# Moving convolution pieces, splitting v's operand and shifting the taps' network in a fused Swin block and dynamic convolution

## The chip, the cores and the metric

The kernel runs on one core of one Trainium2 chip. The metric is the device time of one execution in microseconds (us). The kernel before takes 3256.59 us, the median of three runs (3252.11 to 3258.15). The profiled execution has a span of 3259.7 us. All data are float32.

The engines are named as in the profile: PE is TensorE (PEld is its weight load, which overlaps the matmuls), DVE is VectorE, ACT is ScalarE, POOL is GpSimd and SP is SyncE, which here only issues transfers.

## What is computed

Sixteen images of 192 channels and 56x56 points go through two layers. Layer 0 is a shifted-window transformer block. Layer 1 is a depthwise 3x3 convolution whose weights depend on the image's mean.

```python
# layer 0, per image (windows of 7x7, shift 3, 6 heads of 32)
h   = window(roll(layernorm(x), -3))
qkv = h @ qkv_w + qkv_b
p   = softmax(q k^T * scale + rel_bias + mask)
x1  = x + roll(unwindow((p v) @ proj_w + proj_b), 3)
x2  = x1 + gelu(layernorm(x1) @ fc1_w + fc1_b) @ fc2_w + fc2_b
# layer 1, per image
t   = relu(gamma * (mean_hw(x2) @ w1.T - running_mean) * rsqrt(running_var + eps) + beta)
wt  = (t @ w2.T + b2) * causal_mask          # 4 of the 9 taps of each channel are left
out = depthwise_conv3x3(x2, wt) + bias
```

## The kernel before

An image is cut into four steps. A step is two bands of seven rows, one from each half of the image, so a tile `[128, 2, 392]` holds 128 channels of both halves, and a tile `[128, 392]` holds the last 64 channels with the half in the partition. There are 64 steps. The main loop's round `i` does three things at once: the MLP of step `i-2`, the attention of step `i`, and the projections q, k and v of step `i+1`. A round's matmuls come in this order: MLP layer one (`ph`), statistics (`st`), scores (`sc`), q/k (`pq`, `pe`, `pk`), MLP layer two, wide part (`pf`) with the transposes of the probabilities (`pt`) between its slices, values (`po`), MLP layer two, narrow part (`pf1`), projection (`pp`) mixed with v (`pv`).

PSUM is used as four pairs of banks, A, B, C and D, handed from tile to tile. At the end of a round the pairs are renamed, `pairs = [C, B_, D, A]`. A tile's next user waits until the last reader of the tile before has finished. The program is written in order, and each engine runs its own instructions in the order written.

After the fourth step of an image (its last MLP round) the taps `wt` of the image are computed. In the three rounds that follow, its convolution is done in six pieces, two a round. A piece is one ACT instruction (`conv_begin`) and three DVE instructions (`conv_rest`).

```python
def attention_v_out(pvs):                         # v leaves PSUM, block-diagonal
    for blk, pv in enumerate(pvs):
        ...
        for s in range(2):
            for j in range(2):
                for h in range(2):
                    dst = vbd[j * 64 : j * 64 + N, h].rearrange(...)[:, blk, :, s, :, j, :]
                    f = src[s * 64 : s * 64 + N, h, :, :, j, :]
                    if j == 0:
                        nc.vector.tensor_copy(dst, f)     # L450
                    else:
                        nc.scalar.copy(dst, f)            # L452

def residual(i, pp, pp1):
    ...
    for lo, hi, to in rolls:                      # 2 instructions, L578
        nc.vector.scalar_tensor_tensor(xs, q1[:, :, lo:hi], pb[1], xs, ALU.add, ALU.add)
    for a in range(2):                            # 4 instructions, L582
        for lo, hi, to in rolls:
            nc.vector.scalar_tensor_tensor(xs, q0[:, a, :, lo:hi], pb[0], xs, ALU.add, ALU.add)

def mlp_first(i, yn, hid, ks, between):           # ks = (A, B, C, D, A, B)
    def gelu(f):
        nc.scalar.activation(hid[:, f], phs[f][:, :, :T], AF.Gelu, bias=f1b[:, f : f + 1])  # L596
    for f in range(3):
        take(f); long(dsts[f], wf1, cols(f), y0, True)
    for f in range(3):
        short(dsts[f], wf1, cols(f), y1, False); gelu(f)
    for f in range(3, NFC):
        take(f); short(dsts[f], wf1, cols(f), y1, True)
    between()
    for f in range(3, NFC):
        long(dsts[f], wf1, cols(f), y0, False); gelu(f)

def norm_squares(key, i, side, engine):           # with engine = ACT at a round's end
    nc.scalar.activation(s0, v0, AF.Square)       # L243
    nc.scalar.activation(s1, v1, AF.Square)       # L244
    for h in range(2):
        nc.gpsimd.tensor_tensor(s0[p, h], s0[p, h], s1[p], ALU.add)   # L250

def taps_pool(b):
    nc.vector.tensor_reduce(pooled, sums.pop(b), AX.X, ALU.add)
    x0, x1 = images[b]                            # the rows above the halves
    nc.gpsimd.tensor_copy(x0[:, 0, :], x0[:, IMG, :])                 # L650
    nc.vector.tensor_copy(x1[0:64, 0, :], x1[64:128, HALF, :])
    nc.vector.tensor_copy(x1[64:128, 0, :], x1[0:64, HALF, :])
    return pooled

def taps(b, pooled, k):
    pt = banks(f"t_{b}", k)[:, 0]
    for kc in range(2):
        mm(pt[:, 0:RED], pooled[:, kc].broadcast_to([128, 128]), w1t[:, kc], kc == 0, kc == 1)
    nc.vector.tensor_tensor(tt[:, 0], pt[:, 0:RED], bn[:, 0], ALU.mult)   # L661
    nc.vector.tensor_tensor(tt[:, 0], tt[:, 0], bn[:, 1], ALU.add)
    nc.vector.scalar_tensor_tensor(tw, tt..., 0.0, w2n..., ALU.max, ALU.mult)
    nc.vector.tensor_reduce(wt..., tw, AX.X, ALU.add)
    nc.vector.tensor_tensor(wt, wt, b2t, ALU.add)

def conv_begin(b, wt, n):
    nc.scalar.activation(y, images[b][kc][:, lo : lo + PR], AF.Identity,
                         bias=cb[kc], scale=wt[:, kc, 1:2])               # L683

def conv_rest(b, wt, n, y):
    tap(0, ...); tap(2, ...)                      # L698, DVE
    if n in (3, 5):
        nc.vector.tensor_copy(y[p, LAST - 3 * PR, :], ...)                # L707
    tap(3, ...)                                   # L698
    ... nc.sync.dma_start(out[...], y[...])

for i in range(2, NS + 2):                        # a round
    norm1_scale(i + 1, dvs.pop(0), nc.vector)     # 12 DVE instructions
    ...
    def between():
        for b, wt, n in conv_ready(1):            # first piece of the round
            conv_rest(b, wt, n, conv_begin(b, wt, n))
        singles[0] = banks(f"st_{i}", C)
        keys.update(stats_of(i))
        var.append(norm_vars(keys))               # ACT L280, DVE L282 read st
    mlp_first(i - 2, yns.pop(i - 2), hid, (A, B_, C, D, A, B_), between)
    ...                                           # scores, q/k, MLP layer two
    ys = [(*c, conv_begin(*c)) for c in conv_ready(1)]   # second piece of the round
    ...
    pf1 = mlp_narrow(i - 2, hid, A)
    for c in ys:
        conv_rest(*c)
    mlp_out(i - 2, 1, pf1[:, :T])                 # L641
    pp, pp1, p_narrow, p_rest, p_whole = project(i, o, B_, C)
    p_narrow(); p_rest()
    pvs, v_rest, v_whole = attention_v(i + 1, (D, A)); v_rest()
    p_whole(); residual(i, pp, pp1); v_whole()
    if (i - 2) % STEPS == STEPS - 1:              # the image's last MLP round
        convs.append({"b": b, "n": 0, "wt": taps(b, taps_pool(b), C)})
    attention_v_out(pvs)
    norm_squares(f"2_{i}", i, 1, nc.scalar)
    pairs = [C, B_, D, A]
```

Of the kernel before, what the change touches and what calls it, by code (L numbers as in the profile page):

```python
# [8 lines left out]
F32 = mybir.dt.float32  # L9
AF = mybir.ActivationFunctionType  # L10
ALU = mybir.AluOpType
AX = mybir.AxisListType

DIM, HEADS, HD = 192, 6, 32
C0, C1 = 128, 64
IMG = 56
NTOK = IMG * IMG
WS, SHIFT = 7, 3
NWIN = IMG // WS
N = WS * WS  # L20
T = WS * IMG
PW = 64 + N
HALF = IMG // 2
STEPS = NWIN // 2
HID = 4 * DIM
NFC = HID // 128
RED = DIM // 4
# [9 lines left out]
def tile_swin_then_dynamic_conv(  # L37
# [31 lines left out]
    nc = tc.nc  # L69
# [13 lines left out]
    def banks(name, k):  # L83
        return psum.tile([128, 2, 512], F32, tag=f"pair{k}", name=name)
# [6 lines left out]
    def mm(dst, lhs, rhs, start, stop):  # L91
        nc.tensor.matmul(dst, lhs, rhs, start=start, stop=stop, skip_group_check=True)  # L92
# [108 lines left out]


    kbd = one.tile([128, 3, NWIN, 2, N], F32, tag="kbd", name="kbd")
    vbd = const.tile([128, 2, NWIN, HEADS // 2, 64], F32, tag="vbd", name="vbd")
    prob = [
        const.tile([128, 2 * HEADS, 64], F32, tag=f"prob{i}", name=f"prob{i}") for i in range(4)
    ]
# [229 lines left out]
    def attention_v_out(pvs):  # L437

        for blk, pv in enumerate(pvs):
            src = pv.rearrange("p h (w n) -> p h w n", w=2)[:, :, :, 0:DIM]  # L440
            src = src.rearrange("p h w (g j d) -> p h w g j d", j=2, d=HD)
            for s in range(2):
                for j in range(2):
                    for h in range(2):
                        dst = vbd[j * 64 : j * 64 + N, h].rearrange(
                            "p (b w s) g (j d) -> p b w s g j d", b=2, s=2, j=2
                        )[:, blk, :, s, :, j, :]
                        f = src[s * 64 : s * 64 + N, h, :, :, j, :]
                        if j == 0:
                            nc.vector.tensor_copy(dst, f)  # L450
                        else:
                            nc.scalar.copy(dst, f)  # L452

    def attention_scores(i, q4, q2, ks):

# [62 lines left out]
    def attention_weigh(po, po1, wp, prt):  # L518
        for s in range(2):
            w = wp * 2 + s  # L520
            for a, g in ((0, 0), (0, 1), (1, 0), (1, 1), (0, 2), (1, 2)):

                r, k = (g, a) if g < 2 else (a, 2)
                o = po[:, a] if g < 2 else po1
                at = (g if g < 2 else a) * 64
                mm(
                    o[at : at + 64, w * N : (w + 1) * N],
                    vbd[:, a, w, g, :],
                    prt[:, r, k * PW + s * 64 : k * PW + s * 64 + N],
                    True,  # L530
                    True,
                )
# [17 lines left out]

    def project(i, o, k, k1):

        pp, pp1 = banks(f"pp_{i}", k), banks(f"pp1_{i}", k1)[:, 0]

        def narrow():
            for a in range(2):
                mm(pp1[a * 64 : a * 64 + 64, :T], wp0[:, C0:DIM], o[:, a], True, False)

        def rest():
            for a in range(2):  # L560
                p = slice(a * 64, a * 64 + 64)
                mm(pp[:, a, :T], wp1[p], o[p, 2], True, False)

        def whole():
            mm(pp1[:, :T], wp2, o[:, 2], False, True)
            for a in range(2):
                mm(pp[:, a, :T], wp0[:, 0:C0], o[:, a], False, True)

        return pp, pp1, narrow, rest, whole

    def residual(i, pp, pp1):
        v0, v1 = rows_of(i)
        q1 = pp1[:, :T].rearrange("p (r c) -> p r c", c=IMG)
        q0 = pp[:, :, :T].rearrange("p h (r c) -> p h r c", c=IMG)
        rolls = ((0, IMG - SHIFT, SHIFT), (IMG - SHIFT, IMG, 0))
        for lo, hi, to in rolls:
            xs = v1[:, :, to : to + hi - lo]
            nc.vector.scalar_tensor_tensor(xs, q1[:, :, lo:hi], pb[1], xs, ALU.add, ALU.add)  # L578
        for a in range(2):
            for lo, hi, to in rolls:  # L580
                xs = v0[:, a, :, to : to + hi - lo]
                nc.vector.scalar_tensor_tensor(xs, q0[:, a, :, lo:hi], pb[0], xs, ALU.add, ALU.add)  # L582
# [63 lines left out]
    def taps_pool(b):  # L646
        pooled = small.tile([128, 2, 1], F32, tag="pooled", name=f"pooled_{b}")
        nc.vector.tensor_reduce(pooled, sums.pop(b), AX.X, ALU.add)
        x0, x1 = images[b]
        nc.gpsimd.tensor_copy(x0[:, 0, :], x0[:, IMG, :])  # L650
        nc.vector.tensor_copy(x1[0:64, 0, :], x1[64:128, HALF, :])
        nc.vector.tensor_copy(x1[64:128, 0, :], x1[0:64, HALF, :])
        return pooled

    def taps(b, pooled, k):

        pt = banks(f"t_{b}", k)[:, 0]
        for kc in range(2):
            mm(pt[:, 0:RED], pooled[:, kc].broadcast_to([128, 128]), w1t[:, kc], kc == 0, kc == 1)
        tt = small.tile([128, 1, RED], F32, tag="tt", name=f"tt_{b}", bufs=1)  # L660
        nc.vector.tensor_tensor(tt[:, 0], pt[:, 0:RED], bn[:, 0], ALU.mult)  # L661
        nc.vector.tensor_tensor(tt[:, 0], tt[:, 0], bn[:, 1], ALU.add)
        tw = small.tile([128, 2 * NTAP, RED], F32, tag="tw", name=f"tw_{b}", bufs=1)
        nc.vector.scalar_tensor_tensor(
            tw,
            tt.broadcast_to([128, 2 * NTAP, RED]),
            0.0,
            w2n.rearrange("p k t r -> p (k t) r"),
            ALU.max,
            ALU.mult,  # L670
        )
        wt = small.tile([128, 2, NTAP], F32, tag="wt", name=f"wt_{b}")
        nc.vector.tensor_reduce(
            wt.rearrange("p k (t o) -> p (k t) o", o=1), tw, AX.X, ALU.add
        )
        nc.vector.tensor_tensor(wt, wt, b2t, ALU.add)
        return wt
# [51 lines left out]
    def has(i):  # L729
        return 0 <= i < NS  # L730

    def conv_ready(k):

        ready = []
        while k and convs and "wt" in convs[0]:
            c = convs[0]
            ready.append((c["b"], c["wt"], c["n"]))
            c["n"] += 1
            k -= 1
            if c["n"] == 6:  # L740
                convs.pop(0)
        return ready
# [7 lines left out]
    def tail_of(i, o, kp, kv):  # L750

        pvs, v_rest, v_whole = attention_v(i + 1, kv) if has(i + 1) else (None, None, None)
        if o is not None:
            pp, pp1, narrow, rest, whole = project(i, o, kp, 3)
            narrow()
            rest()
        if pvs:
            v_rest()
        if o is not None:
            whole()  # L760
            residual(i, pp, pp1)
        if pvs:
            v_whole()
            attention_v_out(pvs)
        if o is not None:
            norm_squares(f"2_{i}", i, 1, nc.scalar)
# [59 lines left out]
    for c, at, lo, n, be, bias in (  # L826
# [5 lines left out]
        p = slice(at, at + n)  # L832
# [2 lines left out]
    nc.vector.tensor_scalar(qkb[:, 0:1], qkb[:, 0:1], SCALE, None, ALU.mult)  # L835
    nc.vector.tensor_scalar(qkb[0:64, 2:3], qkb[0:64, 2:3], SCALE, None, ALU.mult)
    nc.vector.tensor_scalar(kb, pick, qkb[:, 1:2], None, ALU.mult)
    for t in [kbd, vbd] + prob:
        nc.gpsimd.memset(t, 0.0)
    keys = stats_of(-1)  # L840
    dev = norm_devs(keys)
# [66 lines left out]
    def taps_weights():  # L908
# [30 lines left out]
        nc.vector.tensor_tensor(m, m, s, ALU.mult)  # L939
        nc.vector.tensor_tensor(m, b, m, ALU.subtract)  # L940
        nc.vector.tensor_scalar(s, s, 1.0 / NTOK, None, ALU.mult)

# [30 lines left out]
    for i in range(2, NS + 2):  # L975
        A, B_, C, D = pairs
        keys = {}


        if has(i + 1):  # L980
            norm1_scale(i + 1, dvs.pop(0), nc.vector)
        if (i + 3) % STEPS == 0 and (i + 3) // STEPS < B:
            b = (i + 3) // STEPS
            images[b] = load_x(b, nc.sync)

        def between():
            for b, wt, n in conv_ready(1):
                conv_rest(b, wt, n, conv_begin(b, wt, n))
            singles[0] = banks(f"st_{i}", C)
            keys.update(stats_of(i))  # L990
            if keys:
                var.append(norm_vars(keys))
# [45 lines left out]
        pf = mlp_wide(i - 2, hid, B_, turn)  # L1038
        mlp_out(i - 2, 0, pf[:, :, :T])
        table(AF.Gelu)  # L1040
        ys = [(*c, conv_begin(*c)) for c in conv_ready(1)]
        if 1 in keys:
            yns[i - 1] = norm2_scale(i - 1, dvs.pop(1))
        if has(i + 3):
# [1 line left out]
        if has(i):  # L1046
            o = attention_rows(i, attention_values(i, prts, D, C))
        pf1 = mlp_narrow(i - 2, hid, A)
        for c in ys:
            conv_rest(*c)  # L1050
        mlp_out(i - 2, 1, pf1[:, :T])
        if has(i):
            pp, pp1, p_narrow, p_rest, p_whole = project(i, o, B_, C)
            p_narrow()
            p_rest()
        if has(i + 1):
# [1 line left out]
            v_rest()  # L1058
        if has(i):
            p_whole()  # L1060
            residual(i, pp, pp1)
        if has(i + 1):
            v_whole()
        if (i - 2) % STEPS == STEPS - 1:
            b = (i - 2) // STEPS
            convs.append({"b": b, "n": 0, "wt": taps(b, taps_pool(b), C)})
        if has(i + 1):
            attention_v_out(pvs)
        if has(i):
            norm_squares(f"2_{i}", i, 1, nc.scalar)  # L1070
        pairs = [C, B_, D, A]
    c = convs.pop()
    for n in range(6):
# [75 lines left out]
```

## Time and profile before

| engine | busy us | share of the span |
|---|---|---|
| PE | 3128.8 | 96% |
| DVE | 2155.5 | 66% |
| ACT | 1855.1 | 57% |
| POOL | 1020.4 | 31% |

Round lengths, measured in the timeline from a round's first `ph` matmul to the next round's, repeat with a period of four:

| round | what it holds besides attention and MLP | length, us |
|---|---|---|
| image's last MLP round | the taps' network, no convolution | 48.61 |
| first after it | pieces 0 and 1 | 49.21 |
| second | pieces 2 and 3 | 47.67, in some images 48.28 to 48.41 |
| third | pieces 4 and 5 | 47.67, in some images 48.28 to 48.45 |

In the profile's lists, "idle before" is time in which an engine stood still just before an instruction, and the name after the arrow is what ended that idle time. In the timeline, each row is a run of alike instructions with its start, its duration, the engine, the source line and the tiles as out<-in. In the sums over stretches of time, PEclk is the share of full clock that TensorE was granted.

### The profile page before, as it was taken

Reading aid. Unit: us, or ns where it says so; the run is one execution under the profiler, and the core shown is the slowest. Engines: PE = TensorE matmul, PEld = TensorE weight load, DVE = VectorE, ACT = ScalarE, POOL = GpSimd, SP = SyncE. Lnnn points to the kernel's source line nnn. Section 1 sums busy time; section 2 is a strip of 40 time slices with the busy share of each in tenths; the row PEclk is TensorE's granted clock in tenths of the full one; section 3 lists DMA queues with packets and bytes.
Section 4 is the critical chain, followed back from the end, with each engine's and each line's share of the span. In section 5 each row is a group of like instructions: output and inputs, shape, how many; then the busy total and the mean of one; then the engine's idle time right before and its main releaser. Section 6 shows DMA issues by size and latency. Waiting matters only on the chain.

```text
span 3259.7 us, 64143 instructions
## 1 busy us (share of the span) xinstructions
PE 3128.8 (96%) x26130; PEld 1938.8 (59%) x26130; DVE 2155.5 (66%) x3893; ACT 1855.1 (57%) x2988; POOL 1020.4 (31%) x912
## 2 busy tenths in 40 slices
PE   5699999999999999999999999999999999999996
PEld 3456566666666656666666656666665666666653
DVE  4345666766767676676776766676676767667664
ACT  2445655655655665565665565565565565566552
POOL 4333233233233223333323323323323323323220
PEclk7699999999999999999999999999999999999998
DMA  3001012121111202102111111202111120201101
GB/s 99 12 19 48 20 40 56 31 60 31 33 53 36 61 26 65 31 26 60 37 51 36 54 29 39 55 30 62 31 32 55 36 59 28 65 25 31 26 31 45
DMA packets 79123, 135.35 MB, mean 42 GB/s; under 512 B 21766, under 2 KB 61692, under 8 KB 76908
## 3 DMA queue, kind: packets, MB, share of 16 engines
q1 hardware_dynamic: 77266, 128.54, 14.0%
q8 instruction: 206, 3.38, 0.4%
q0 software_dynamic: 1056, 1.92, 0.3%
q10 hardware_dynamic: 506, 0.79, 0.1%
q14 instruction: 89, 0.73, 0.1%
HBM read 41.25 MB, written 38.54 MB: 24 GB/s over the span
## 4 chain that ended last, share of the span: by engine, by line
PE 89%; DVE 4%; ACT 2%; issue 1%; POOL 0%; DMA 0%; ACTq 0%; DVEq 0%; POOLq 0%
PE ph L92 23%; PE pf L92 22%; PE pv L92 7%; PE pp L92 7%; PE po L92 5%; PE pq L92 4%; PE pt L509 4%; PE sc L92 4%; PE st L92 4%; PE pe L92 4%; PE pk L92 4%; DVE y L698 1%; DVE vbd L450 1%; DVE y L707 1%; ACT vbd L452 1%
## 5 line engine op out<-in xcount | busy, mean ns | idle before, releaser
L92 PE MATMUL ph<-yn,wf 128*128 128x392 f32 (+1 forms) x3072 | 811.4, 501 | 27.3 <-ACT vbd L452 18.8
L92 PE MATMUL pf<-hid,wf 128*128 128x392 f32 (+1 forms) x3072 | 802.8, 494 | 3.5 <-ACT hid L596 2.0
L496 POOL TENSOR_TENSOR prob<-e,tot 113x588 f32<-113x588 f32 x256 | 298.1, 1176 | 1165.8 <-DVE tot L495 1151.3
L92 PEld LDWEIGHTS ph<-yn,wf 128*128 128x128 f32 (+1 forms) x3072 | 425.4, 189 | 384.4 <-issue 91.6
L452 ACT COPY vbd<-pv 49x192 f32<-49x192 f32 x512 | 135.4, 312 | 768.1 <-DVE vbd L450 767.8
L92 PEld LDWEIGHTS pf<-hid,wf 128*128 128x128 f32 (+1 forms) x3072 | 386.4, 164 | 303.6 <-issue 119.9
L698 DVE SCALAR_TENSOR_TENSOR y<-x,wt,y 128x770 f32<-128x770 f32 x288 | 321.0, 1116 | 214.8 <-ACT y L683 208.1
L596 ACT ACTIVATE hid<-ph,f1b 128x784 f32<-128x784 f32 x384 | 336.8, 912 | 127.7 <-PE ph L92 127.3
L250 POOL TENSOR_TENSOR sq<-sq,sq 64x392 f32<-64x392 f32 x256 | 262.9, 1027 | 383.1 <-ACT sq L244 368.6
L347 POOL TENSOR_TENSOR yn<-x,dv 128x784 f32<-128x784 f32 x64 | 129.2, 2019 | 574.6 <-DMA dv<-dev 541.8
L92 PEld LDWEIGHTS pv<-wqkv,win 64*128 64x128 f32 (+1 forms) x2048 | 259.4, 190 | 47.5 <-DVE x L641 7.7
L92 PE MATMUL pv<-wqkv,win 64*128 64x192 f32 (+1 forms) x2048 | 277.1, 328 | 7.7 <-DVE x L641 4.4
L480 DVE TENSOR_TENSOR e<-sc,bias_t 113x588 f32<-113x588 f32 x256 | 179.6, 763 | 149.5 <-PE sc L92 149.4
L487 DVE TENSOR_TENSOR e<-e,top 113x588 f32<-113x588 f32 x256 | 265.7, 1038 | 8.9
L641 DVE SCALAR_TENSOR_TENSOR x<-pf,cols,x 128x784 f32<-128x784 f32 (+1 forms) x128 | 105.8, 827 | 232.8 <-PE pf L92 225.7
L92 PE MATMUL pp<-o,wp 128*128 128x392 f32 (+2 forms) x896 | 253.0, 517 | 2.6 <-ACT o L545 2.6
L235 ACT ACT_TABLE_LOAD x192 | 246.3, 1283 | 3.4
L515 ACT COPY prt<-pt 128x678 f32<-128x678 f32 x256 | 179.1, 726 | 118.1 <-PE pt L509 116.5
L490 ACT ACTIVATE e<-e 113x588 f32<-113x588 f32 x256 | 176.7, 691 | 107.6 <-DVE e L487 105.2
L450 DVE COPY vbd<-pv 49x192 f32<-49x192 f32 x512 | 159.2, 349 | 97.0 <-ACT vbd L452 82.9
L509 PEld LDWEIGHTS pt<-ident,prob 113*128 113x128 f32 x1536 | 167.3, 142 | 76.1 <-issue 47.0
L92 PE MATMUL po<-prt,vbd 128*64 128x49 f32 x6144 | 199.9, 225 | 0.2 <-ACT prt L515 0.2
(143 smaller groups left out, 4073.3 us busy)
## 6 DMA issues: line engine op xcount, KB each, us to landing
dv<-dev SPq DMA_DIRECT2D x1020, 49.0 KB
x<-in_x_dram SPq DMA_DIRECT2D x15, 1484.0 KB
out_dram<-y SPq DMA_DIRECT2D x48, 392.0 KB
out_dram<-y SPq DMA_DIRECT2D x48, 196.0 KB
x<-in_x_dram SPq DMA_DIRECT2D x16, 392.0 KB
x<-in_x_dram SPq DMA_DIRECT2D x15, 350.0 KB
out_dram<-y SPq DMA_DIRECT2D x16, 308.0 KB
out_dram<-y SPq DMA_DIRECT2D x16, 154.0 KB
```

The source lines that it names most:

```text
L92: nc.tensor.matmul(dst, lhs, rhs, start=start, stop=stop, skip_group_check=True)
L235: nc.scalar.activation(junk, eps_t[0:1], func)
L250: nc.gpsimd.tensor_tensor(s0[p, h], s0[p, h], s1[p], ALU.add)
L450: nc.vector.tensor_copy(dst, f)
L480: nc.vector.tensor_tensor(e, sc[:PW, :, : HEADS * N], rel, ALU.add)
L487: nc.vector.tensor_tensor(ehs[wp], ehs[wp], t.broadcast_to([PW, 2 * HEADS, N]), ALU.subtract)
L490: nc.scalar.activation(es[wp], es[wp], AF.Exp)
L496: nc.gpsimd.tensor_tensor(prob[wp][:PW, :, 0:N], ehs[wp], t.broadcast_to([PW, 2 * HEADS, N]), ALU.mult)
L509: nc.tensor.transpose(pt[:, a, g * PW : (g + 1) * PW], prob[wp][:PW, h : h + 2, :].rearrange("p h k -> p (h k)"), ident[:PW, :PW],)
L515: nc.scalar.copy(prt, pt[:, :, : 3 * PW])
L596: nc.scalar.activation(hid[:, f], phs[f][:, :, :T], AF.Gelu, bias=f1b[:, f : f + 1])
L698: nc.vector.scalar_tensor_tensor(dst, src, wt[:, kc, t : t + 1], dst, ALU.mult, ALU.add)
```

## The change

Five things are altered.

- **Convolution.** Both pieces of a round are begun on ACT at the top of the round, ahead of the first GELU, and their DVE part follows `norm1_scale` directly. The piece beside the narrow part of MLP layer two and the one in `between` are gone from there.
- **v's operand.** The tile `vbd` becomes two tiles, one per image half. DVE copies half 0 and ACT copies half 1, where before each took one position `j` of both halves.
- **Taps' network.** Its matmuls move from behind v to between the projection and the second part of v, and write the unused bank of the projection's narrow pair. The first DVE instruction on them stands inside `residual`, the rest stands behind the copies of v and the squares.
- **Batch norm scale.** It is folded into `w1t` at the start, so one DVE instruction for each image is gone.
- **Rows above the halves.** The three copies (one POOL, two DVE) move to the very end of the round, behind `norm_squares`.

The change is meant to take work off the stretches in which TensorE waits on ACT or DVE at the end of a round.

```diff
-    vbd = const.tile([128, 2, NWIN, HEADS // 2, 64], F32, tag="vbd", name="vbd")
+    vbd = [
+        const.tile([128, NWIN, HEADS // 2, 64], F32, tag=f"vbd{h}", name=f"vbd{h}")
+        for h in range(2)
+    ]
...
-            for s in range(2):
-                for j in range(2):
-                    for h in range(2):
-                        dst = vbd[j * 64 : j * 64 + N, h].rearrange(
+            for h, copy in enumerate((nc.vector.tensor_copy, nc.scalar.copy)):
+                for s in range(2):
+                    for j in range(2):
+                        dst = vbd[h][j * 64 : j * 64 + N].rearrange(
...
-                        f = src[s * 64 : s * 64 + N, h, :, :, j, :]
-                        if j == 0:
-                            nc.vector.tensor_copy(dst, f)
-                        else:
-                            nc.scalar.copy(dst, f)
+                        copy(dst, src[s * 64 : s * 64 + N, h, :, :, j, :])
...
-    def residual(i, pp, pp1):
+    def residual(i, pp, pair1, between=None):
...
             nc.vector.scalar_tensor_tensor(xs, q1[:, :, lo:hi], pb[1], xs, ALU.add, ALU.add)
+        if between:
+            between()
         for a in range(2):
...
     def taps_pool(b):
         pooled = small.tile([128, 2, 1], F32, tag="pooled", name=f"pooled_{b}")
         nc.vector.tensor_reduce(pooled, sums.pop(b), AX.X, ALU.add)
+        return pooled
+
+    def taps_rows(b):
+
         x0, x1 = images[b]
         nc.gpsimd.tensor_copy(x0[:, 0, :], x0[:, IMG, :])
         nc.vector.tensor_copy(x1[0:64, 0, :], x1[64:128, HALF, :])
         nc.vector.tensor_copy(x1[64:128, 0, :], x1[0:64, HALF, :])
-        return pooled
...
+    def taps_hidden(b, pt):
         tt = small.tile([128, 1, RED], F32, tag="tt", name=f"tt_{b}", bufs=1)
-        nc.vector.tensor_tensor(tt[:, 0], pt[:, 0:RED], bn[:, 0], ALU.mult)
-        nc.vector.tensor_tensor(tt[:, 0], tt[:, 0], bn[:, 1], ALU.add)
+        nc.vector.tensor_tensor(tt[:, 0], pt[:, 0:RED], bn[:, 1], ALU.add)
+        return tt
+
+    def taps_out(b, tt):
         tw = small.tile([128, 2 * NTAP, RED], F32, tag="tw", name=f"tw_{b}", bufs=1)
...
+        for k in range(2):
+            nc.vector.tensor_tensor(w1t[:, k], w1t[:, k], s, ALU.mult)
...
+        ys = [(*c, conv_begin(*c)) for c in conv_ready(2)]
         if has(i + 1):
             norm1_scale(i + 1, dvs.pop(0), nc.vector)
+        for c in ys:
+            conv_rest(*c)
...
         def between():
-            for b, wt, n in conv_ready(1):
-                conv_rest(b, wt, n, conv_begin(b, wt, n))
             singles[0] = banks(f"st_{i}", C)
...
-        ys = [(*c, conv_begin(*c)) for c in conv_ready(1)]
...
-        for c in ys:
-            conv_rest(*c)
         mlp_out(i - 2, 1, pf1[:, :T])
...
             p_whole()
-            residual(i, pp, pp1)
+        b, pt, at = (i - 2) // STEPS, None, lambda: None
+        if (i - 2) % STEPS == STEPS - 1:
+            pt = taps(b, taps_pool(b), pair1[:, 1] if has(i) else banks(f"t_{b}", C)[:, 0])
+            convs.append({"b": b, "n": 0})
+
+            def at():
+                convs[-1]["tt"] = taps_hidden(b, pt)
+
+        if has(i):
+            residual(i, pp, pair1, at)
+        else:
+            at()
         if has(i + 1):
             v_whole()
-        if (i - 2) % STEPS == STEPS - 1:
-            b = (i - 2) // STEPS
-            convs.append({"b": b, "n": 0, "wt": taps(b, taps_pool(b), C)})
-        if has(i + 1):
             attention_v_out(pvs)
         if has(i):
             norm_squares(f"2_{i}", i, 1, nc.scalar)
+        if pt is not None:
+            convs[-1]["wt"] = taps_out(b, convs[-1]["tt"])
+            taps_rows(b)
```

More of the change, by code (lines that the diff above doesn't have):

```diff
@@ L527, in attention_weigh @@
                     o[at : at + 64, w * N : (w + 1) * N],
-                    vbd[:, a, w, g, :],
+                    vbd[a][:, w, g, :],
                     prt[:, r, k * PW + s * 64 : k * PW + s * 64 + N],
@@ L551, in project @@
     def project(i, o, k, k1):
-        pp, pp1 = banks(f"pp_{i}", k), banks(f"pp1_{i}", k1)[:, 0]
+        pp, pair1 = banks(f"pp_{i}", k), banks(f"pp1_{i}", k1)
+        pp1 = pair1[:, 0]
         def narrow():
@@ L567, in whole @@
                 mm(pp[:, a, :T], wp0[:, 0:C0], o[:, a], False, True)
-        return pp, pp1, narrow, rest, whole
-    def residual(i, pp, pp1):
+        return pp, pair1, narrow, rest, whole
+    def residual(i, pp, pair1, between=None):
         v0, v1 = rows_of(i)
-        q1 = pp1[:, :T].rearrange("p (r c) -> p r c", c=IMG)
+        q1 = pair1[:, 0, :T].rearrange("p (r c) -> p r c", c=IMG)
         q0 = pp[:, :, :T].rearrange("p h (r c) -> p h r c", c=IMG)
@@ L652, in taps_pool, with taps @@
         nc.vector.tensor_copy(x1[64:128, 0, :], x1[0:64, HALF, :])
-        return pooled
-    def taps(b, pooled, k):
-        pt = banks(f"t_{b}", k)[:, 0]
+    def taps(b, pooled, pt):
         for kc in range(2):
             mm(pt[:, 0:RED], pooled[:, kc].broadcast_to([128, 128]), w1t[:, kc], kc == 0, kc == 1)
+        return pt
+    def taps_hidden(b, pt):
         tt = small.tile([128, 1, RED], F32, tag="tt", name=f"tt_{b}", bufs=1)
-        nc.vector.tensor_tensor(tt[:, 0], pt[:, 0:RED], bn[:, 0], ALU.mult)
-        nc.vector.tensor_tensor(tt[:, 0], tt[:, 0], bn[:, 1], ALU.add)
+        nc.vector.tensor_tensor(tt[:, 0], pt[:, 0:RED], bn[:, 1], ALU.add)
+        return tt
+    def taps_out(b, tt):
         tw = small.tile([128, 2 * NTAP, RED], F32, tag="tw", name=f"tw_{b}", bufs=1)
@@ L753, in tail_of @@
         if o is not None:
-            pp, pp1, narrow, rest, whole = project(i, o, kp, 3)
+            pp, pair1, narrow, rest, whole = project(i, o, kp, 3)
             narrow()
@@ L760, in tail_of @@
             whole()
-            residual(i, pp, pp1)
+            residual(i, pp, pair1)
         if pvs:
@@ L837, in tile_swin_then_dynamic_conv @@
     nc.vector.tensor_scalar(kb, pick, qkb[:, 1:2], None, ALU.mult)
-    for t in [kbd, vbd] + prob:
+    for t in [kbd] + vbd + prob:
         nc.gpsimd.memset(t, 0.0)
@@ L1048, in tile_swin_then_dynamic_conv @@
         pf1 = mlp_narrow(i - 2, hid, A)
-        for c in ys:
-            conv_rest(*c)
         mlp_out(i - 2, 1, pf1[:, :T])
         if has(i):
-            pp, pp1, p_narrow, p_rest, p_whole = project(i, o, B_, C)
+            pp, pair1, p_narrow, p_rest, p_whole = project(i, o, B_, C)
             p_narrow()
@@ L1060, in tile_swin_then_dynamic_conv @@
             p_whole()
-            residual(i, pp, pp1)
+        b, pt, at = (i - 2) // STEPS, None, lambda: None
[8 more added lines that the diff above has]
+            at()
         if has(i + 1):
             v_whole()
-        if (i - 2) % STEPS == STEPS - 1:
-            b = (i - 2) // STEPS
-            convs.append({"b": b, "n": 0, "wt": taps(b, taps_pool(b), C)})
-        if has(i + 1):
             attention_v_out(pvs)
```

## The prediction, made before the changed kernel ran

> **What bounds the kernel now.** I read the page's first part and its chain first.
>
> ```profile
> PE 3128.8 (96%) x26130; PEld 1938.8 (59%) x26130; DVE 2155.5 (66%) x3893; ACT 1855.1 (57%) x2988; POOL 1020.4 (31%) x912
> PE 89%; DVE 4%; ACT 2%; issue 1%; POOL 0%; DMA 0%; ACTq 0%; DVEq 0%; POOLq 0%
> ```
>
> PE is busy 96% of the span and makes 89% of the chain that ended last. No work on PE is removed, so the change can only win back PE's waits, or add some. Next, the waits:
>
> ```profile
> ACT vbd L452 <- DVE vbd L450: 767.8, 254, 13.2
> ...
> PE ph L92 <- ACT vbd L452: 18.8, 16, 3.3
> ...
> PEld pv L92 <- DVE x L641: 7.7, 11, 0.8
> ...
> PE ph L92 <- DVE tt L661: 5.9, 15, 0.4
> ```
>
> The columns are total us, times, longest. The first line is large, but it is idle time of ACT, which is not the bound. The three others are PE's: two of them once per image, at the taps, and one 11 times, at v (the weight load's wait, 7.7 us in all). The timeline around one image's taps shows the first two in their place:
>
> ```profile
> 1529.18 2.76 PE L92 MATMUL pv<-wqkv,win 128*128 128x192 f32 x16
> 1529.38 1.41 DVE L582 SCALAR_TENSOR_TENSOR x<-pp,cols,x 128x371 f32<-128x371 f32 x4 [0.56 <-PE pp L92]
> ...
> 1532.71 2.87 PE L92 MATMUL ph<-yn,wf 128*128 128x392 f32 x8 [0.39 <-DVE tt L661]
> ...
> 1536.70 5.90 PE L92 MATMUL ph<-yn,wf 128*128 128x392 f32 x28 [1.11 <-ACT vbd L452]
> ...
> 1539.36 0.51 ACT L244 ACTIVATE sq<-x 128x392 f32<-128x392 f32 x1
> ...
> 1539.90 2.52 ACT L596 ACTIVATE hid<-ph,f1b 128x784 f32<-128x784 f32 x3
> 1539.95 2.17 POOL L250 TENSOR_TENSOR sq<-sq,sq 64x392 f32<-64x392 f32 x2 [6.88 <-ACT sq L244]
> ```
>
> The reader is to see the two PE waits (0.39 and 1.11 us), and that L250 on POOL runs a good 2 us after ACT's squares, beside the GELUs. From round lengths: 47.67 us is the floor. The taps' round has 48.61 - 47.67 = 0.94 too much (four `t` matmuls and the wait on tt), the first round after it 49.21 - 47.67 = 1.54 (the wait on vbd). Eleven of the second and third rounds have 0.6 to 0.8 too much, the v wait. The 14 images in the middle of the loop average 193.73 us for four rounds, against 4 x 47.67 = 190.68. So the change can gain at most about 3 us an image, 46 us in 15 images.
>
> **What the Trainium skill says.** "TensorE: Matmul & The Clock Gate", section "Architectural detail", states that ACT and DVE take instructions strictly first in, first out. This agrees: no ACT or DVE instruction overtakes one in this trace, and POOL's do not either. The same page, section "What's actually happening", describes a clock gate that halves PE's clock after an idle window of 3.41 us, windows running free. In this trace less idleness was enough:
>
> ```profile
> core 0: us, PE busy (x) PEld busy (x) DVE busy (x) ACT busy (x) POOL busy (x), PEclk, DMA share, GB/s
> ...
> 3201.00:3204.40 3.40, 1.12 (x6) 0.37 (x3) 1.47 (x3) 0.00 (x0) 2.39 (x2) 0.99 0.36 89
> 3204.40:3207.80 3.40, 3.40 (x7) 1.80 (x6) 0.00 (x0) 0.00 (x0) 1.42 (x2) 0.50 0.09 29
> ```
>
> PE was idle 2.28 of 3.40 us, and the next window ran at 0.50: seven matmuls instead of some 16, a loss of half a window, 1.7 us. "SBUF — State Buffer", section "Who interferes with whom", says DVE and POOL share a port pair that one instruction holds whole. This agrees: the 56-element copy L707 takes 187 ns at best, 1901 ns at worst.
>
> **The change, part by part.**
>
> *Both pieces in layer one, ordinary rounds.* ACT: three pieces' `conv_begin` took 2.90 us at the end of the run, so one costs about 0.93 in a row. In the round whose `ph` starts at 1049.49, ACT's squares end at 1054.09 and the first GELU starts at 1054.53, waiting for PE. The split vbd lets DVE's eight copies run without handshakes, about 0.27 us apart: 1048.41 to 1050.93 (before: 1052.2). In the built program ACT's copies of a block still carry a wait on DVE's last copy of that block, so ACT ends at 1051.98 instead of 1052.79, and the squares at about 1053.25. Two `conv_begin` end at 1055.1: the first GELU is 0.55 us late, the third ends at 1057.6, and `st`, which reuses its bank pair, starts at 1057.68 anyhow. Lost: 0 to 0.1 us. DVE: `norm1_scale` (4.6 us) ends at about 1055.6, six taps of 1.056 at 1062.0, L282 (1.14) at 1063.2, with 0.2 more for an L707. Scores reuse L282's bank pair and start at 1063.94: no wait. The round stays at 47.67.
>
> *The second piece leaves the narrow part.* There L707 collided with POOL and delayed L641, which v waits on. This goes: 11 times 0.6 to 0.8, **-7.4 us**.
>
> *Taps beside the projection.* The four `t` matmuls cost about 0.40 us (0.11 apart), and tt no longer ends a PE wait: the taps' round becomes 48.07, **-0.54 an image**. The wait on vbd at the third `ph` group (-1.1 to -1.5) should go too. But the projection's narrow pair now also holds `t`, and in the built program L578 waits for the last `t` matmul, so DVE's residual moves from 1528.07 to about 1529.8, 1.7 us later.
>
> *First round after the taps: the new wait.* The first `conv_begin` reads row 0 of the image. POOL's copy of that row now stands behind L250, which waits for both ACT squares. ACT is in order, so the GELUs stand behind `conv_begin`. Worked out in the shown stretch:
> - residual 1529.8, tt, L582 end: about 1531.9.
> - DVE's vbd copies 1531.9 to 1534.2; ACT's second block from 1534.3 to 1535.25.
> - squares (0.76 + 0.51) to 1536.55.
> - POOL L250 2.17, row copy 0.23: 1539.1.
> - two `conv_begin`: 1539.15 to 1541.05. First GELU (0.91) ends at 1541.96, third at 1543.6.
> - PE: `ph` starts at 1532.2 (0.5 earlier). Its fifth group, which reuses the first GELU's bank pair, is due 6.8 us later at 1538.96 and starts at about 1542.05, a stand of 3.1 us. `st` follows at 1543.65 instead of 1540.37.
>
> So the round has **3.28** too much instead of 1.54. DVE (taps' rest, rows, `norm1_scale`, six taps, L282) ends at about 1548.1, before the scores at 1549.9, and adds nothing.
>
> *Sum without the clock.* Four rounds: 2 x 47.67 + 48.07 + 50.95 = 194.36, against 193.73: +0.63 an image, +9.5 us for 15. Removed tt instruction, last image's taps and the faster v copies in the first rounds: about -2. The stand ahead of the fifth group leaves PE idle for about 2.95 us at a stretch. Against windows of 3.41 us, the worst window is idle by 1.5 to 2.95 us depending on where it falls. The shown dip needed 2.28 or less; the wait of 1.1 us here caused none. I estimate three in four rounds get a half-clock window: 0.75 x 1.7 x 15 = **+19 us**. Total: 3256.6 + 9.5 - 2 + 19 = 3283, rounded to 3282.
>
> **Rivals.**
> 1. *The waits simply go.* If POOL's row copy came in time, an image would need 2 x 47.67 + 48.07 + 47.7 = 191.1, a gain of 2.6 x 15 = 39 us, 3217. For it: every wait of PE in the list that the change names is removed. Against it: the order on POOL and ACT is fixed, and its links are durations from this trace.
> 2. *The stand stays, the clock holds.* If an idle share of two thirds in one window is needed and the stand falls across two windows, or is shorter than worked out, only +7.5 remains: 3264.
> 3. *DVE becomes the bound of layer one.* L282 with 0.7 us in hand could hold up the scores if POOL's L250 slowed more of `norm1_scale`. Half a microsecond in 45 rounds would be +22: 3304 with the rest. Against it: POOL is idle after L250.
>
> **Range and chances.** Without any dip and with a stand of 2.3 us the time is about 3250; with a dip in each of the 15 rounds and 0.1 us at each late GELU it is 3293 to 3303. Range 3257 to 3303. A gain of 2% (under 3191) is more than all PE waits outside the start. A loss of 2% (over 3322) would need rival 3 on top. Chances: 0.01, 0.96, 0.03.
>
> **What would show it.** In the waits: "PE ph <- ACT hid" some 15 times at about 3 us; ACT y waiting for POOL's x copy; no "PE ph <- DVE tt", no "pv <- DVE x". Round lengths near 48.1, 51 (52.6 with a dip), 47.7, 47.7. PEclk 0.50 for one window after most of the stands. In the trace, vbd on ACT ends about 0.8 us earlier. Wrong would be: rounds after the taps near 47.7 (rival 1), or second and third rounds over 48 with "PE sc <- DVE dev" (rival 3).

## The result and the profile after

The changed kernel takes 3345.55 us (median of four runs, 3340.33 to 3346.89), against 3257.37 us before in the same runs: a ratio of 1.0271, 95% interval 1.0253 to 1.0289. It is 88 us slower. The prediction, 3282 us with a range up to 3303, had the direction and the largest of the places, the first round after the taps. It missed the size by 63 us.

The page after, busy time and chain:

```profile
PE 3166.4 (95%) x26130; PEld 1943.5 (58%) x26130; DVE 2110.2 (63%) x3879; ACT 1887.9 (56%) x2988; POOL 998.1 (30%) x913
PE 73%; ACT 6%; POOL 5%; DVE 5%; issue 4%; SPq 2%; DMA 1%; ACTq 0%; DVEq 0%; POOLq 0%
```

PE has the same 26130 matmuls and is busy 38 us longer: that is no more work but slower matmuls. Between the first round's start and the last round's, the granted clock is at half for 25 stretches of 3.41 us, against 2 before. PE's share of the chain fell from 89% to 73%, and ACT, POOL and DVE came in. The waits after (total us, times, longest):

```profile
ACT vbd L451 <- DVE vbd L451: 700.3, 128, 11.8
...
PE ph L92 <- ACT hid L598: 77.1, 44, 4.3
...
ACT y L692 <- POOL x L656: 44.8, 15, 3.0
```

The waits on tt, on vbd in mid-loop, and at v are gone, as the change wanted. In their place PE waits 44 times for a GELU: 15 times about 4.3 us, once in each first round after the taps, and 29 times under 0.5 us, in the second and third rounds. The last line gives the cause of the 15: ACT stands 3.0 us ahead of the first convolution piece, for POOL's row copy. The timeline of one first round after the taps:

```profile
1565.69 2.95 DVE L451 COPY vbd<-pv 49x192 f32<-49x192 f32 x8
1566.06 6.95 PE L92 MATMUL ph<-yn,wf 128*128 128x392 f32 x28
1567.24 1.29 ACT L451 COPY vbd<-pv 49x192 f32<-49x192 f32 x4 [11.75 <-DVE vbd L451]
...
1568.73 1.28 ACT L451 COPY vbd<-pv 49x192 f32<-49x192 f32 x4 [0.20 <-DVE vbd L451]
...
1570.81 0.51 ACT L247 ACTIVATE sq<-x 128x392 f32<-128x392 f32 x1
...
1571.39 2.54 POOL L253 TENSOR_TENSOR sq<-sq,sq 64x392 f32<-64x392 f32 x2 [4.85 <-ACT sq L247]
...
1574.00 0.27 POOL L656 COPY x<-x 128x56 f32<-128x56 f32 x1
...
1574.31 1.97 ACT L692 ACTIVATE y<-x,cols,wt 128x784 f32<-128x784 f32 x2 [2.99 <-POOL x L656]
...
1576.30 2.52 ACT L598 ACTIVATE hid<-ph,f1b 128x784 f32<-128x784 f32 x3
1577.27 2.98 PE L92 MATMUL ph<-yn,wf 64*128 64x392 f32 x8 [4.26 <-ACT hid L598]
```

Read downwards, each link ends where the next begins: copies of v, squares on ACT, their sum on POOL, the row copy, two `conv_begin`, the GELU, and only then PE's fifth `ph` group. The last row also shows eight matmuls in 2.98 us, which take 1.73 us in an ordinary round (below). The sums over stretches of that time (length, then busy us with instruction counts by engine, then PEclk) show the clock:

```profile
core 0: us, PE busy (x) PEld busy (x) DVE busy (x) ACT busy (x) POOL busy (x), PEclk, DMA share, GB/s
...
1572.90:1576.30 3.40, 0.11 (x2) 0.00 (x0) 2.90 (x10) 1.97 (x2) 1.31 (x2) 1.00 0.00 0
1576.30:1579.70 3.40, 2.43 (x8) 1.18 (x8) 3.29 (x5) 2.52 (x3) 0.00 (x0) 0.50 0.09 32
1579.70:1583.10 3.40, 3.40 (x22) 0.99 (x24) 1.82 (x2) 0.00 (x0) 0.00 (x0) 0.50 0.42 163
```

The stand (PE's idle time ahead of its fifth group) emptied one stretch of 3.4 us, and the next two ran at half clock. This came after all 15 stands: seven times for one stretch, eight times for two.

The second and third rounds lose in another way. They have no row copy, and ACT doesn't wait for POOL there. An ordinary round before and one after:

```profile
1049.49 8.26 PE L92 MATMUL ph<-yn,wf 128*128 128x392 f32 x36
...
1052.26 0.53 ACT L452 COPY vbd<-pv 49x192 f32<-49x192 f32 x2 [0.70 <-DVE vbd L450]
...
1054.53 2.52 ACT L596 ACTIVATE hid<-ph,f1b 128x784 f32<-128x784 f32 x3 [0.44 <-PE ph L92]
```

```profile
1420.84 6.95 PE L92 MATMUL ph<-yn,wf 128*128 128x392 f32 x28
...
1422.80 1.29 ACT L451 COPY vbd<-pv 49x192 f32<-49x192 f32 x4 [0.21 <-DVE vbd L451]
...
1425.29 1.96 ACT L692 ACTIVATE y<-x,cols,wt 128x784 f32<-128x784 f32 x2
...
1427.28 2.52 ACT L598 ACTIVATE hid<-ph,f1b 128x784 f32<-128x784 f32 x3
1428.24 1.73 PE L92 MATMUL ph<-yn,wf 64*128 64x392 f32 x8 [0.46 <-ACT hid L598]
```

ACT ends its copies of v 3.30 us after the round's first `ph` matmul before, and 3.25 us after it now. The two `conv_begin` come on top, so the first GELU starts after 6.44 us instead of 5.04, and PE waits for it.

Mean round lengths over the 14 images in the middle of the loop:

| round | before | predicted | after |
|---|---|---|---|
| image's last MLP round | 48.61 | 48.07 | 48.12 |
| first after it | 49.23 | 50.95, 52.6 with a dip | 54.40 |
| second | 47.87 | 47.67 | 48.55 |
| third | 48.02 | 47.67 | 48.55 |
| sum | 193.73 | 194.36 without dips | 199.62 |

The difference of the sums, 5.9 us, times 15 images is 88 us, the whole loss.

### The profile page after: what moved, and what is told of

It is laid out like the page before. It is cut to its first block, busy times and chain, and to the rows that moved or that the text cites. A ratio compares the mean times of both kernels' runs of the same rounds, so it can differ in the third digit from the quotient of the medians.

```text
span 3345.1 us, 64108 instructions
## 1 busy us (share of the span) xinstructions
PE 3166.4 (95%) x26130; PEld 1943.5 (58%) x26130; DVE 2110.2 (63%) x3879; ACT 1887.9 (56%) x2988; POOL 998.1 (30%) x913
## 4 chain that ended last, share of the span: by engine, by line
PE 73%; ACT 6%; POOL 5%; DVE 5%; issue 4%; SPq 2%; DMA 1%; ACTq 0%; DVEq 0%; POOLq 0%
PE pf L92 20%; PE ph L92 16%; PE pp L92 6%; PE po L92 5%; PE pq L92 4%; PE st L92 4%; PE sc L92 4%; PE pt L508 4%; PE pe L92 4%; PE pk L92 4%; PE pv L92 3%; DVE vbd L451 2%; ACT y L692 2%; SPq L309 2%; POOL sq L253 2%
## 5 line engine op out<-in xcount | busy, mean ns | idle before, releaser
L92 PE MATMUL ph<-yn,wf 128*128 128x392 f32 (+1 forms) x3072 | 840.2, 518 | 82.9 <-ACT hid L598 77.1
L451 ACT COPY vbd<-pv 49x192 f32<-49x192 f32 x512 | 160.1, 313 | 704.9 <-DVE vbd L451 700.3
L707 DVE SCALAR_TENSOR_TENSOR y<-x,wt,y 128x770 f32<-128x770 f32 x288 | 313.5, 1103 | 21.0 <-ACT y L692 13.3
L350 POOL TENSOR_TENSOR yn<-x,dv 128x784 f32<-128x784 f32 x64 | 119.0, 1859 | 578.4 <-DMA dv<-dev 556.2
L92 PEld LDWEIGHTS po<-prt,vbd 128*64 128x64 f32 x6144 | 191.0, 139 | 9.4 <-ACT prt L514 0.6
```

The source lines that it names most:

```text
L451: copy(dst, src[s * 64 : s * 64 + N, h, :, :, j, :])
L707: nc.vector.scalar_tensor_tensor(dst, src, wt[:, kc, t : t + 1], dst, ALU.mult, ALU.add)
```

## The experiments

Each ratio is against the kernel before, timed on the same chip.

**One instruction of the change moved back.** POOL's row copy goes back behind the pooled sum, ahead of the squares.

```diff
 def taps_pool(b):
     nc.vector.tensor_reduce(pooled, sums.pop(b), AX.X, ALU.add)
+    x0 = images[b][0]
+    nc.gpsimd.tensor_copy(x0[:, 0, :], x0[:, IMG, :])
     return pooled
 def taps_rows(b):
-    nc.gpsimd.tensor_copy(x0[:, 0, :], x0[:, IMG, :])
     ...
```

> The changed kernel with one instruction moved: POOL copies the image's row 0 right after the pooled sum, ahead of POOL's part of the squares, as before the change. Theory A (the order on POOL and ACT holds up the first convolution piece and with it the GELUs): the first conv_begin no longer waits for POOL, it starts when ACT's squares end, 3 us earlier; the first GELU's bank pair comes free about 1.5 us too late instead of 4.3, there is no half-clock window, the first round after the taps takes about 49.3 us instead of 53.8 to 55.1, the others stay at 48.55 and 48.12: about 3268 us. Theory B (two conv_begin ahead of the GELUs and the slower copies of v alone make the stand): first round stays over 53 us, 3340.

Measured: 3273.74 us, ratio 1.0048 (1.0031 to 1.0064). First rounds take 49.63 us (one of 15: 51.64; the last, in the shorter work of the loop's end: 48.95), the others 48.55 and 48.12, and no stand is followed by half clock. One first round in its timeline:

```profile
957.00 1.96 ACT L693 ACTIVATE y<-x,cols,wt 128x784 f32<-128x784 f32 x2
957.18 2.54 POOL L253 TENSOR_TENSOR sq<-sq,sq 64x392 f32<-64x392 f32 x2 [6.22 <-ACT sq L247]
...
958.99 2.52 ACT L598 ACTIVATE hid<-ph,f1b 128x784 f32<-128x784 f32 x3
959.95 1.73 PE L92 MATMUL ph<-yn,wf 64*128 64x392 f32 x8 [1.16 <-ACT hid L598]
```

`conv_begin` now starts before POOL's squares do, PE stands 1.16 us instead of 4.26, and the eight matmuls take 1.73 us. The place of one copy of 0.27 us costs 72 of the 88 us. Theory B falls. The other 16 us remain, and the second and third rounds are as slow as in the change.

**Convolution alone.** The kernel before with both pieces begun at the top of the round, nothing else.

```diff
+        ys = [(*c, conv_begin(*c)) for c in conv_ready(2)]
         norm1_scale(i + 1, dvs.pop(0), nc.vector)
+        for c in ys:
+            conv_rest(*c)
 ...                       # both old places emptied, as in the change
```

> The kernel before with only the convolution moved: both pieces begun ahead of the GELUs. Row copy early, v's operand one tile, taps where they were. Theory A: the second and third rounds become 48.55 us as in the changed kernel, since there ACT ends its copies of v 3.3 us after the first ph matmul with either split; the first round after the taps is about 51.3 us (49.21 plus 2.05 for the late GELUs), more if a half-clock window comes; together 3305 to 3330. If the late row copy is the whole loss of the change (theory C), second and third rounds stay at 47.7 and the time is near 3257.

Measured: 3304.84 us, ratio 1.0149 (1.0134 to 1.0164). First rounds take 51.08 us, second and third 48.60, taps' rounds 48.61, and no stand in a first round is followed by half clock. The waits have a new line:

```profile
PE ph L92 <- ACT hid L596: 39.1, 44, 1.7
```

So the early pieces lose by themselves, in every round that has them, with the row copy early and v's operand undivided. Theory C falls: second and third rounds did not stay at 47.7.

**Taps alone.** The kernel before with the taps' part of the change, its late row copy included.

```diff
-            pp, pp1, p_narrow, p_rest, p_whole = project(i, o, B_, C)
+            pp, pair1, p_narrow, p_rest, p_whole = project(i, o, B_, C)
 ...                       # taps into pair1[:, 1], rest behind norm_squares, as in the change
```

> The kernel before with only the taps' network moved (matmuls beside the projection, rest and row copies behind the squares, norm scale folded); convolution and v's operand as before. Theory A: the late row copy does no harm here, because the first conv_begin stands behind the first three GELUs and has room; the taps' round is 48.12, the first after it about 47.8, the others as before: about 3229 us, faster than both kernels. Theory D (the taps' move itself delays the end of the round, since the residual waits for its matmuls): first round after it 49 us or more, 3250 or more.

Measured: 3221.94 us, ratio 0.9893 (0.9878 to 0.9907), faster than both kernels. First rounds take 47.68 us, taps' rounds 48.12. The late copy harms nothing here: the first piece stands behind three GELUs, and first rounds are at the floor. Theory D falls: the residual's later start is hidden. What remains over the floor is the wait at v, eight times in this profile.

**v's operand alone.** The kernel before with two tiles for v, one per image half.

```diff
-            for s in range(2):
-                for j in range(2):
-                    for h in range(2):
+            for h, copy in enumerate((nc.vector.tensor_copy, nc.scalar.copy)):
+                for s in range(2):
+                    for j in range(2):
...                       # the tiles and their reader accordingly
```

> The kernel before with only v's operand as two tiles, one per image half. Theory A (copies of one engine in a row that change partitions do not overlap, 0.37 us apart on DVE and 0.32 on ACT): ordinary rounds stay at 47.67, since ACT ends its copies at the same time as before; after the taps PE waits 0.4 us longer on v's first block, first round 49.6; about 3262 us. Rival: two engines reading one PSUM pair at a time slow each other; same time here, but the spacing in ordinary rounds is seen in the trace. If the split helped as meant, first round 48.5 and 3245.

Measured: 3257.28 us, ratio 1.0004 (0.9996 to 1.0013): no gain. First rounds take 49.43 us, 0.2 more than before. The split as it stands does nothing for the end of the round. This run alone does not tell theory A from its rival; the next two do.

**v's operand by block.** The first experiment's kernel, but DVE copies windows 0 to 3 and ACT windows 4 to 7, each into its own tile, with the image halves in the inner loop.

```diff
-            for h, copy in enumerate((nc.vector.tensor_copy, nc.scalar.copy)):
-                for s in range(2):
-                    for j in range(2):
-                        dst = vbd[h][j * 64 : j * 64 + N]...
+            copy = (nc.vector.tensor_copy, nc.scalar.copy)[blk]
+            for s in range(2):
+                for j in range(2):
+                    for h in range(2):
+                        dst = vbd[blk][j * 64 : j * 64 + N, h]...
...                       # the tiles' shape and reader accordingly
```

> The changed kernel with the row copy early (as in e1) and v's operand split by block of four windows instead of by image half: DVE copies block 0, ACT block 1, in pairs of the two halves of one partition range, so neither engine waits for the other. Theory A: copies of a pair overlap again (DVE 0.27 us apart, ACT 0.22), ACT ends about 2.4 us after the first ph matmul instead of 3.25, the GELUs are in time: second and third rounds 47.7 instead of 48.55. First round about 49.4, held by DVE (scores wait for the statistics). About 3245 us. Theory E (the slower spacing comes from both engines reading PSUM at once): copies stay 0.32 and 0.37 us apart, second and third rounds 48.2 or more, 3258.

Measured: 3239.37 us, ratio 0.9949 (0.9933 to 0.9966). Second and third rounds take 47.68 us, first rounds 49.42, held by DVE as expected (PE's scores wait 15 times for the statistics, up to 1.6 us). The copies of one round in its timeline:

```profile
1373.32 2.53 DVE L452 COPY vbd<-pv 49x192 f32<-49x192 f32 x8
1374.59 2.15 ACT L452 COPY vbd<-pv 49x192 f32<-49x192 f32 x8 [10.33 <-PE pv L92]
```

Eight copies on ACT take 2.15 us, where the changed kernel needs 1.29 and 1.28 with a wait on DVE between. Within a pair (same partitions, the two halves) they start 0.22 us apart on ACT and 0.26 to 0.28 on DVE, between pairs 0.32 and 0.35 to 0.37. Theory E falls: both engines read PSUM at once here, and pairs still overlap.

**The same with the loops in the other order.** Only the loop over halves moves outwards.

```diff
-            for s in range(2):
-                for j in range(2):
-                    for h in range(2):
+            for h in range(2):
+                for s in range(2):
+                    for j in range(2):
```

> The kernel of e5 with one edit: the loop over the image halves is the outer one, so that no two copies in a row of an engine have the same partitions. Theory A (a change of partitions keeps copies from overlapping): 0.37 us apart on DVE and 0.32 on ACT again, second and third rounds about 48.0, 3256. Theory E: spacing as in e5, same time as e5.

Measured: 3259.93 us, ratio 1.0015 (1.0006 to 1.0023), 20.6 us more than the run before. Second and third rounds take 48.09 us. The same copies:

```profile
1382.96 2.92 DVE L452 COPY vbd<-pv 49x192 f32<-49x192 f32 x8
1384.23 2.59 ACT L452 COPY vbd<-pv 49x192 f32<-49x192 f32 x8 [10.33 <-PE pv L92]
```

The same sixteen copies take 0.4 us longer on either engine, because each now starts on other partitions than the one before it. A change of PSUM bank isn't what makes a step slow: in the run before, the fast step within a pair changes the bank, and so does the slow step between two pairs. Neighbours that keep both partitions and bank occur in no run, so that case is not shown.

**A stand of middle length.** The changed kernel, row copy late, with v's operand by block (the edit to the copies of the fifth experiment alone).

> The changed kernel with v's operand split by block, row copy late as in the change. Theory A: the chain squares, POOL, row copy, conv_begin, GELU stays but starts 1.3 us earlier; the stand ahead of the fifth ph group is about 2.9 us instead of 4.3. First round about 51.0 us, 52.7 where a half-clock window follows; with a stand between e1's 1.2 and the change's 4.3 this shows how long a stand brings one. Second and third rounds 47.7. 3262 to 3290.

Measured: 3267.36 us, ratio 1.0036 (1.0023 to 1.0049). The stand is 2.7 us in each first round. Ten of 15 take 50.80 us; three take 52.04 to 52.29, one 53.63, and the last image's 51.26, and these five have a dip in the clock of one or two stretches. The stretch with the stand and the one after it, in two rounds without a dip and two with one:

```profile
core 0: us, PE busy (x) PEld busy (x) DVE busy (x) ACT busy (x) POOL busy (x), PEclk, DMA share, GB/s
560.20:563.60 3.40, 1.60 (x10) 0.58 (x6) 3.30 (x12) 2.03 (x3) 1.25 (x2) 1.00 0.00 0
563.60:567.00 3.40, 2.49 (x20) 1.02 (x24) 3.33 (x4) 2.47 (x3) 0.00 (x0) 1.00 0.00 0
...
1533.00:1536.40 3.40, 1.39 (x10) 0.49 (x6) 3.30 (x12) 2.24 (x3) 1.04 (x2) 1.00 0.01 2
1536.40:1539.80 3.40, 2.70 (x8) 1.19 (x8) 3.33 (x4) 2.26 (x3) 0.00 (x0) 0.51 0.00 0
```

With PE busy 1.60 of 3.40 us the clock holds, with 1.39 it halves. In both cases PE waits some 2.7 us, and what differs is where the stand falls against the stretches. Over all 15 first rounds, the five with a dip are the five in which PE was busy for 0.40 of such a stretch or less.

**What the runs point to.** Taps beside the projection, row copy early, v by block; early convolution only in the second and third round.

```diff
+        late = not (convs and convs[0]["n"])          # first round after the taps
-        ys = [(*c, conv_begin(*c)) for c in conv_ready(2)]
+        ys = [(*c, conv_begin(*c)) for c in conv_ready(0 if late else 2)]
 ...                       # conv_ready(int(late)) in the two old places
```

> What the runs so far point to: taps beside the projection, row copy early, v's operand by block; convolution pieces of the first round after the taps where they were before the change, those of the second and third round in layer one. Theory A: no wait of PE at the taps, at v, or at the GELUs; rounds 48.12, 47.7, 47.7, 47.7; about 3216 us, faster than both kernels and than e3 (3222), whose remaining 0.7 us waits at v it takes away.

Measured: 3212.97 us, ratio 0.9869 (0.9854 to 0.9883). Every mid-loop round is at 47.68, or 48.12 with the taps. PE's longest waits are now all from the start of the program:

```profile
PE singles L143 <- DMA cols_rows<-in_L_conv_qkv_b_dram: 9.6, 1, 9.6
PE pt L509 <- ACT prt L515: 9.2, 2, 6.3
PE pq L92 <- DVE top L486: 9.1, 1, 9.1
```

The same three parts that cost 88 us together are worth 42 us (3254.83 against 3212.97) once the row copy, the grouping of v's copies and the first round's convolution are put right.

## Why the prediction was wrong

- **Right: what bounds the kernel.** PE does, and its waits and its clock are what moved. The eighth experiment gained 42 us, where the prediction put the most to be gained at 46 us.
- **Right: the taps.** 48.12 against 48.07 worked out. Together with the wait on vbd that is (0.49 + 1.55) x 15 = 31 of the 35 us that the third experiment gained.
- **Right: the mechanism in the first round after the taps**, link by link: squares, POOL, row copy, `conv_begin`, GELU, then half clock. Rival 1 (the waits simply go) failed for the reason given against it, and rival 2 (the clock holds) because all 15 stands brought half clock. For the second and third rounds it does not hold: there the prediction put the loss at 0 to 0.1 us.
- **Wrong: the step "DVE's eight copies run without handshakes, about 0.27 us apart"** (a handshake is a wait of ACT and DVE on each other), and with it "the first GELU is 0.55 us late" and "Lost: 0 to 0.1 us" in ordinary rounds. The spacing was read from pairs of copies in the kernel before, which lie on the same partitions. The change breaks up the pairs, and the spacing becomes 0.35 to 0.39 us on DVE and 0.32 instead of 0.22 on ACT. DVE's eight copies took 2.95 us where 2.52 were worked out. ACT's last four, which wait for them, lost another 0.3. So ACT's copies ended 3.25 us after the first `ph` matmul, not 2.5, no earlier than before, and the two pieces pushed the GELUs out. "Lost: 0 to 0.1 us" was 0.88 us, in 30 rounds: **26 us missed**. The fifth and sixth experiments show that the order of the copies by itself costs 0.41 us of such a round (48.09 against 47.68). That ACT's wait on DVE makes up the rest of the 0.88 is read from the timeline and not tested by itself.
- **Wrong in size: the stand of 3.1 us.** It measured 4.26. The slower copies gave 0.9 of the difference, and POOL's squares took 2.54 instead of 2.17. By the undipped rounds of the seventh experiment, where a stand of 2.7 us made the round 3.12 longer than the floor, 4.26 is worth some 4.7 over the floor, where 3.28 was worked out: **about 21 us missed** in 15 rounds.
- **Wrong in size: the clock, +19 us.** Three in four stands with one half-clock stretch were assumed. All 15 had one, and eight of them two. The first rounds average 54.40 us, about 2.0 more than the 52.4 the stand alone would give: 31 us, **about 12 missed**.

These sum to 59 of the 63 us. How the last two share their 33 us is an estimate, since the stand alone, without half clock, was not measured at 4.26 us. The prediction's own sum was 3283, put down as 3282.

Rival 3 (DVE holds the scores) did not take place in the change. The prediction's sign for it was second and third rounds over 48 with PE waiting on DVE; these rounds came, at 48.55, but with PE waiting on ACT. In first rounds it showed where the stand was shorter: the scores waited up to 0.3 us for DVE in the first experiment, and up to 1.6 us in the fifth, where the stand was gone.

## What to carry to other kernels

When work moves ahead on an in-order engine, follow what its first instruction reads back through every queue: here a copy of 0.27 us, placed behind another queue's work, cost 72 us. Take the spacing of a run of small instructions only from a run in the same order, and keep neighbours on the same partitions. Count a stand of TensorE by how much of a stretch of 3.4 us it empties, too, and not by its own length alone.

## What the runs showed of the hardware that was not expected

- The granted clock in these traces changes on a grid of 3.41 us. In the main loops of all ten profiles, every stretch at full clock in which PE was busy for 0.40 of it or less was followed by half clock (27 of 27), and none with 0.45 or more was. A full idle stretch, as the Trainium skill has it ("TensorE: Matmul & The Clock Gate", section "What's actually happening"), isn't needed.
- In these runs, copies from PSUM on ACT and DVE overlap with the one before only on the same partitions: 0.22 against 0.32 us apart on ACT, 0.26 to 0.28 against 0.35 to 0.39 on DVE, with the same durations of 0.31 and 0.35 us.
- At half clock, all nine stretches in these loops that were busy for 0.53 to 0.80 of their length were followed by a second one, and all 34 with 0.83 or more by full clock. Counted as work at full clock, busy time at half clock is worth half: 0.80 becomes 0.40 and 0.83 becomes 0.41. By this estimate the way back to full clock takes no more work than staying there, where the runs leave the limit open between 0.40 and 0.45. Two cases of the seventh experiment, busy for 0.80 and for 0.83, each with the stretch after it:

```profile
core 0: us, PE busy (x) PEld busy (x) DVE busy (x) ACT busy (x) POOL busy (x), PEclk, DMA share, GB/s
...
1536.43:1539.84 3.41, 2.74 (x8) 1.19 (x8) 3.34 (x4) 2.23 (x3) 0.00 (x0) 0.50 0.00 0
1539.84:1543.26 3.42, 3.42 (x22) 0.99 (x24) 2.45 (x3) 0.00 (x0) 0.00 (x0) 0.50 0.31 117
...
758.19:761.60 3.41, 2.82 (x8) 1.19 (x8) 3.34 (x4) 2.15 (x3) 0.00 (x0) 0.50 0.00 0
761.60:765.00 3.40, 3.40 (x30) 1.47 (x29) 2.37 (x3) 0.97 (x2) 0.00 (x0) 1.00 0.33 125
```
